# Values of an attention kernel: one wide matmul over the high and low half of the weights, and another order in the first steps

## Chip, cores and metric

One core of a Trainium2 chip. The metric is the device time of one execution in microseconds (us); lower is better. All numbers of this document come from executions on that chip and from a hardware profile of one of them. Engines: PE is TensorE (matmul), PEld its weight loads, DVE VectorE, ACT ScalarE, POOL GpSimd, SP SyncE.

## What is computed

The reference, cut to what matters (4 batches of 512 tokens, model width 512, 16 heads of 128, FFN width 1408, all float32):

```python
xn = layernorm(x)
q = einsum('bpd,hde->bphe', xn, W_Q) + b_Q        # k and v alike
scores = einsum('bqhe,bkhe->bhqk', q, k) / sqrt(128)
attn = softmax(where(causal, scores, -1e5))
z = einsum('bkhe,bhqk->bqhe', v, attn)
s = einsum('bqhe,hed->bqd', z, W_O) + b_O
hdn = silu((xn @ gate_w.T) * gate_s) * ((xn @ up_w.T) * up_s)
g = silu((hdn @ down_w.T) * down_s)
out = x + s * g
```

## The kernel before

**Numbers.** TensorE multiplies in a reduced-width float32 (fp32r). Every operand is therefore kept as a pair: `hi`, the value rounded to fp32r, and `lo`, the rest. A product takes three matmuls, hi·hi, lo·hi and hi·lo, that add into the same PSUM tile (`mm3`, L91, and `mm3_all`, L96). The class `Split` holds such a pair. ACT makes `hi` by a copy that rounds, and DVE or POOL makes `lo` by a subtraction.

**Stages.** First the attention of all heads, then the FFN. The attention loop (L594) goes over 64 steps `n`, in the order group of two heads (`g`, 8 of them), batch (`b`, 4), head in the group (`i`, 2). Everything stands in one order written out by hand (`manual_schedule`), and each engine works its own queue in that order. A step holds, for TensorE: the scores `sc` of this head (`softmax`, L305), a part of side work (`fill`, L607), the projections `psq` and `psk` of the next head (`project`, L278), and `z` = attention times values of the head before (`attend`, L418), then the rest of the side work. The side work at `i == 0` is the values of this group and batch, one tile of 128 tokens at a time (`project_v`, L270, two in the first half of the step, two in the second); at `i == 1` it is the output projection `pso` of the group and batch before (`project_out`, L469).

**Values.** `project_v` makes the 128 tokens times 256 columns (two heads) of a group: 12 matmuls with x's hi or lo as the stationary operand and 256 columns of the weights `wv` as the moving one. Then ACT copies the high half out of PSUM (L274) and DVE subtracts it for the low half (L275). The PSUM tile is one of five buffers of the pool `ps_mm`, which `psq`, `psk`, `z`, `pso` and half of the x transposes `tr` share.

**Softmax.** DVE adds the mask and takes the maximum (L331), ACT takes the exponential (L345), DVE the reciprocal of the sum (L348), POOL multiplies (L351). Then the probabilities are transposed: DVE turns blocks of 32 (L365, `turn_p`), and a trip through DRAM on the SP queue (`turn`, `ptr`) puts the blocks in place. In the next step `split_p` (L387) splits them: ACT makes hi (L398), and the low part is made in two halves (L400), from step 9 on one by POOL and one by DVE.

**Weights.** `prepare` (L176) starts a load and notes when it is due; `split_pending(n)` (L166) splits what is due, by a copy on ACT (L150) and a subtraction on POOL (L151).

**First steps.** Layer norm is `ln_stats` (DVE), `ln_sd` (ACT), `ln_normalize` (DVE) and `ln_transposes`, PE transposes `tr` that are put between the matmuls of `project_v` through the list `side`. Batch 0 is made ahead of the loop, and batch `b + 1` in the second half of the step `(g, i) == (0, 0)` of batch `b`. The statistics of batch 1 are made in two calls, one tile ahead of the loop (L580) and three in step 0 (L661).

**End.** `down` (L792) makes the last projection, 128 tokens at a time, and stores the result on the SP queue. The last tile is made in two halves.

Of the kernel before, what the change touches and what calls it, by code (L numbers as in the profile page):

```python
# [18 lines left out]
P = 128  # L19
# [24 lines left out]
def kernel(  # L44
# [67 lines left out]
    with ExitStack() as at:  # L112
# [70 lines left out]
                prepare(when, flat(d[h]), src[h].rearrange("p c e -> p (c e)"), f"{n}r{h}")  # L183

        def prepare_v(g, due):
            wv[g] = weight(wvop, [P, ND, HG * E], f"wv{g}", "wv")
            half = ND // 2
            for i in range(2):
                c = slice(i * half, (i + 1) * half)
                src = w_v[g][:, c, :].rearrange("p c e -> p (c e)")  # L190
                prepare(due, flat(wv[g][:, c, :]), src, f"wvr{g}_{i}")
# [10 lines left out]
        def ln_stats(b, tt, only=None, mv=None):  # L202

            todo = list(enumerate(tt))
            if only is not None:
                todo = todo[:only] if mv is None else todo[only:]
            if mv is None:
                mv = small.tile([P, len(tt), 2], F32, name="mv")
            for k, t in todo:
                st = small.tile([P, 6], F32, name="st")  # L210
                nc.vector.bn_stats(out=st, in_=x_in[b, t])
                nc.vector.bn_aggr(out=mv[:, k, :], in_=st)
            mv_of[b, tuple(tt)] = mv
            return mv
# [53 lines left out]
        v_of = {}  # L268

        def project_v(g, b, t):  # L270
            ps = ps_mm.tile([P, HG * E], F32, name="psv", tag="mm")
            mm3_all(ps, [(xnT[b][:, c, ts(t, P)], wv[g][:, c, :]) for c in range(ND)])
            v = weight(vp, [P, HG * E], f"v{g}_{b}_{t}", "v")
            nc.scalar.copy(v.hi, ps)  # L274
            nc.vector.tensor_tensor(v.lo, ps, v.hi32, ALU.subtract)  # L275
            v_of.setdefault((g, b), []).append(v)

        def project(b, h, w, bias, name, parts=1):  # L278
# [247 lines left out]
        with tc.manual_schedule():  # L526
# [23 lines left out]
            ln_transpose(0, 1)  # L550
            split_pending(-3)
            wv_lows = split_pending(-2, None)
            mv = ln_stats(0, [2, 3], 1)
            ln_low(0, 0)
            ln_low(0, 1)
            ln_stats(0, [2, 3], 1, mv)
            ln_sd(0, [2, 3])
            table(AF.Exp)
            ln_normalize(0, 2)
# [10 lines left out]
            ln_low(0, 2)  # L570
            ln_low(0, 3)
            project_v(0, 0, 0)
            next(q_of)
            next(k_of)
            qT = next(q_of)
            kT = next(k_of)
            split_pending(-1)
            for t in range(NT):
                load_x(1, t)
            mv = ln_stats(1, range(NT), 1)  # L580
            bo_bc = load_const(b_o.broadcast_to([P, D]), [P, D], "bo_bc")
            ds_bc = load_const(down_s.broadcast_to([P, D]), [P, D], "ds_bc")

# [10 lines left out]
            for n, (g, b, i) in enumerate(heads):  # L594
# [11 lines left out]

                def fill(ks):  # L607
                    for t in ks:
                        if i == 0 and not (n == 0 and t == 0):
                            project_v(g, b, t)  # L610
                        if i == HG - 1 and prev is not None:
                            project_out(*prev, t, zs[prev])
# [7 lines left out]
                of = softmax(qT, kT, norms if n > 0 else [])  # L620
                if n > 1 and early:
                    pt = split_p(raw, B * HG < n < len(heads) - 2)
                if n > 0:
                    while norms:
                        norms.pop(0)()
                look()
                half = NT // 2 if nxt is not None else NT - 1
                fill(range(0, half))
                if nxt is not None:
                    raw_next = turn_p(of)  # L630
                if not early:
# [7 lines left out]
                        load_acc(*prev, t)  # L639
                if nxt is None:  # L640

                    for k, tag in enumerate(("wvh", "wvl")):
                        two = wvop.tile([P, 2, D], F32, name=f"a_last{k}", tag=tag)
                        for t in range(2):
                            load_acc(g, b, 2 * k + t, two[:, t, :])
                per_g = B * HG
                if (b, i) == (0, HG - 1):
                    prepare_o(g, n + 1)
# [9 lines left out]
                    load_look()  # L658
                if nxt is not None:
                    if n == 0:  # L660
                        ln_stats(ln_b, range(NT), 1, mv)  # L661
                    elif ln_b is not None and n != 1:
                        ln_stats(ln_b, range(NT))
                    nh = nxt[0] * HG + nxt[2]
                    *_, qT = project(nxt[1], nh, wq[nh], bq_sb, "q")
                    if n == 0:
                        ln_sd(ln_b, range(NT))
                        table(AF.Exp)
                    while norms:
                        norms.pop(0)()  # L670
                if nxt is not None:
                    *_, kT = project(nxt[1], nh, wk[nh], bk_sb, "k")
                    raw = raw_next
                if before is not None:
                    attend_last(before, pt)
# [5 lines left out]
                if ln_next:  # L681
                    side.extend([lambda: None] * (2 * ND))
                    for t in range(NT):
                        side.extend(ln_transposes(b + 1, t))
                        side.append(lambda t=t: ln_low(b + 1, t))
                    fill(range(half, NT))
                    split_pending(n)
                    while side:
                        side.pop(0)()
                    if b + 2 < B:  # L690
                        for t in range(NT):
                            load_x(b + 2, t)
# [19 lines left out]
    def ffn(exact):  # L712
        with ExitStack() as ff:
# [75 lines left out]
                    nc.sync.dma_start(out=xt, in_=x[b, ts(t, P), :])  # L789
                    tail_in[b, t] = a, xt  # L790

            def down(b, t, parts=1):  # L792
                if not exact:
                    load_tail(b, [t])
                a, xt = tail_in.pop((b, t))
                o = fp.tile([P, D], F32, name="o")
                for k in range(parts):
                    c = ts(k, D // parts)
                    pd = ps_d.tile([P, D // parts], F32, name="pd")
                    for f in range(NF):  # L800
                        w = Split(wd[f].hi[:, c], None if exact else wd[f].lo[:, c])
                        mm(pd, hid[b][f][:, ts(t, P)], w, False, f == 0, f == NF - 1)
                    nc.vector.tensor_tensor(o[:, c], pd, ds_bc[:, c], ALU.mult)  # L803
                    nc.scalar.activation(o[:, c], o[:, c], AF.Silu)  # L804
                    nc.vector.tensor_tensor(o[:, c], o[:, c], a[:, c], ALU.mult)
                    nc.vector.tensor_tensor(o[:, c], o[:, c], xt[:, c], ALU.add)
                    nc.sync.dma_start(out=out[b, ts(t, P), c], in_=o[:, c])

            with tc.manual_schedule():
                for b in range(B):  # L810
                    for f in range(NF):
                        gate_up(b, f)
                        if f == 0 and b > 0:
                            for t in range(NT):
                                down(b - 1, t)
                    if exact:
                        load_tail(b, range(NT))
                for t in range(NT):
                    down(B - 1, t, 2 if t == NT - 1 else 1)

    flag = nc.values_load(inexact, min_val=0, max_val=P * LOW_BITS)
    with tc.If(flag == 0) as cond:
# [62 lines left out]
```

## Time and profile before

| | |
|---|---|
| median of 3 runs | 1213.09 us (1212.78 to 1213.54) |
| the profiled execution | 1212.96 us, of which 1211.2 us lie between its first and last instruction (its span) |
| granted TensorE clock | 0.999 of full speed |
| PE busy | 1198.4 us, 99% of the span |
| DVE, ACT, POOL busy | 792.5, 549.3, 379.1 us (65%, 45%, 31%) |
| values (`psv`) in the chain that ended last | 14% of the span |

A row of a timeline gives the start of a group of equal instructions in us, their time from the first start to the last end, the engine, the line of the kernel, and the tiles. Matmuls are pipelined: one still drains while the next streams, so what a group costs TensorE is the distance from its start to the start of the next group, not its own length. Idle time of an engine and what ended it stands in square brackets.

### The profile page before, as it was taken

The numbers are of one execution on the slowest core, as the hardware profiler recorded it, in microseconds if no ns is written. First come the engines' busy times: TensorE is split into PE (matmuls) and PEld (weight loads), VectorE is DVE, ScalarE is ACT, GpSimd is POOL, SyncE is SP. The second block draws the span as 40 slices with busy tenths as digits, with TensorE's granted clock in tenths as the row PEclk, the third lists the DMA queues.
The fourth block names the chain that finished last, engine by engine and source line by source line (L and its number), as shares of the span: only waits on it lengthen the run. The fifth ranks groups of instructions, "written<-read, shape, count | busy, mean of one in ns | idle before, by whom it ended". The sixth has DMA issues, their size and how long they took to land.

```text
span 1211.2 us, 19214 instructions
## 1 busy us (share of the span) xinstructions
PE 1198.4 (99%) x6466; PEld 1045.7 (86%) x6466; DVE 792.5 (65%) x2149; ACT 549.3 (45%) x1272; POOL 379.1 (31%) x484
## 2 busy tenths in 40 slices
PE   8999999999999999999999999999999999999997
PEld 8888888888888888888888888888888888888886
DVE  7987777777777767777776666667667543443443
ACT  6654444455454445454544454445444331323231
POOL 3222332343234324332523252325231350212010
PEclk9999999999999999999999999999999999999999
DMA  5464455756666667666655555555555892727241
GB/s 180 129 189 155 134 174 191 209 175 199 203 207 197 199 195 220 189 197 194 200 185 180 188 182 174 175 174 182 184 168 168 273 296 79 218 78 223 75 146 38
DMA packets 117913, 215.55 MB, mean 178 GB/s; under 512 B 13232, under 2 KB 45744, under 8 KB 117808
## 3 DMA queue, kind: packets, MB, share of 16 engines
q1 hardware_dynamic: 74016, 134.51, 35.0%
q10 hardware_dynamic: 29376, 53.26, 14.3%
q0 software_dynamic: 14416, 26.48, 8.0%
q8 instruction: 53, 0.87, 0.3%
q14 instruction: 52, 0.43, 0.1%
HBM read 135.17 MB, written 79.04 MB: 177 GB/s over the span
## 4 chain that ended last, share of the span: by engine, by line
PE 94%; issue 2%; DVE 2%; DMA 1%; POOL 1%; ACT 0%; SPq 0%; ACTq 0%; POOLq 0%; DVEq 0%
PE psv L104 14%; PE psq L104 14%; PE psk L104 13%; PE z L432 8%; PE sc L104 8%; PE pd L748 7%; PE pg L748 7%; PE pu L748 7%; PE pso L92 5%; PE pso L93 5%; PE pso L94 5%; PE sc L322 1%; PE z L435 1%; DMA wqr<-in_w_q 1%; DVE sq L365 0%
## 5 line engine op out<-in xcount | busy, mean ns | idle before, releaser
L351 POOL TENSOR_SCALAR p<-p,rtot 128x512 f32<-128x512 f32 (+3 forms) x256 | 149.9, 604 | 591.8 <-DVE rtot L348 570.4
L345 ACT ACTIVATE p<-p,nmax 128x512 f32<-128x512 f32 (+3 forms) x256 | 140.9, 553 | 111.5 <-DVE nmax L331 111.5
L365 DVE STREAM_TRANSPOSE sq<-p 128x256 f32<-128x256 f32 x378 | 113.2, 361 | 0.1
L104 PE MATMUL sc<-k,q 128*128 128x512 f32 (+2 forms) x576 | 111.8, 338 | 0.6 <-ACT k L288 0.6
L104 PEld LDWEIGHTS sc<-k,q 128*128 128x128 f32 x576 | 98.9, 188 | 11.4 <-ACT k L288 0.8
L288 ACT ACTIVATE q<-psq,consts 128x512 fp32r<-128x512 f32 (+1 forms) x65 | 44.4, 682 | 122.4 <-PE psq L104 49.7
L331 DVE CUSTOM_DVE_ANT_0 p<-sc,mask 128x512 f32<-128x512 f32 (+2 forms) x192 | 96.2, 551 | 0.1
L289 DVE SCALAR_TENSOR_TENSOR k<-psk,consts,k 128x512 fp32r<-128x512 f32 (+1 forms) x65 | 48.1, 739 | 72.1 <-ACT k L288 72.1
L400 POOL TENSOR_TENSOR pt<-ptr,pt 128x640 fp32r<-128x640 f32 x53 | 83.6, 1577 | 9.7 <-ACT pt L398 9.5
L398 ACT CAST pt<-ptr 128x640 fp32r<-128x640 f32 x126 | 85.0, 724 | 0.3 <-DMA ptr<-turn 0.2
L288 ACT ACTIVATE k<-psk,consts 128x512 fp32r<-128x512 f32 (+1 forms) x65 | 44.2, 679 | 89.8 <-PE psk L104 89.8
L289 DVE SCALAR_TENSOR_TENSOR q<-psq,consts,q 128x512 fp32r<-128x512 f32 (+1 forms) x65 | 47.9, 737 | 49.2 <-ACT q L288 47.5
L774 DVE SCALAR_TENSOR_TENSOR hd<-pu,consts,sg 128x512 f32<-128x512 f32 x44 | 33.0, 751 | 65.8 <-PE pu L748 61.1
L478 DVE TENSOR_TENSOR a<-pso,a 128x512 f32<-128x512 f32 x108 | 69.4, 681 | 0.0
L348 DVE RECIPROCAL rtot<-tot 128x1 f32<-128x1 f32 x256 | 41.4, 162 | 41.3 <-ACT p L345 35.2
L400 DVE TENSOR_TENSOR pt<-ptr,pt 128x640 fp32r<-128x640 f32 x73 | 66.8, 925 | 0.9 <-ACT pt L398 0.9
L432 PE MATMUL z<-pt,v_0h 128*128 128x512 f32 x128 | 50.5, 394 | 0.0
L345 ACT ACTIVATION_READ_ACCUMULATOR p<-p,nmax 128x1 f32 x256 | 47.9, 187 | 0.0
L432 PE MATMUL z<-pt,v_1h 128*128 128x384 f32 x128 | 44.2, 345 | 0.0
L804 ACT ACTIVATE o<-o 128x512 f32<-128x512 f32 (+1 forms) x17 | 10.3, 607 | 68.8 <-DVE o L803 68.8
L772 ACT ACTIVATE sg<-pg,consts 128x512 f32<-128x512 f32 x44 | 30.3, 688 | 17.4 <-PE pg L748 17.4
L432 PE MATMUL z<-pt,v_2h 128*128 128x256 f32 x128 | 35.9, 280 | 0.0
(758 smaller groups left out, 3270.8 us busy)
## 6 DMA issues: line engine op xcount, KB each, us to landing
turn<-sq SPq DMA_DIRECT2D x63, 640.0 KB, 3.5
ptr<-turn SPq DMA_DIRECT2D x252, 160.0 KB, 3.4
acc<-a SPq DMA_DIRECT2D x124, 256.0 KB, 3.1
a<-acc ACTq DMA_DIRECT2D x108, 256.0 KB, 2.9
xt<-in_x SPq DMA_DIRECT2D x16, 256.0 KB, 4.2
wor<-in_w_o ACTq DMA_DIRECT2D x16, 256.0 KB, 4.6
fa<-acc SPq DMA_DIRECT2D x16, 256.0 KB, 6.4
fx<-in_x SPq DMA_DIRECT2D x16, 256.0 KB, 6.6
```

Source lines behind the costliest of these rows:

```text
L104: nc.tensor.matmul(ps, l, r, start=n == 0, stop=n == len(todo) - 1)
L288: nc.scalar.activation(q.hi[:, at_], ps, AF.Identity, bias=bias[:, h : h + 1])
L289: nc.vector.scalar_tensor_tensor(q.lo[:, at_], ps, bias[:, h : h + 1], q.hi32[:, at_], ALU.add, ALU.subtract)
L331: nc.vector.tensor_tensor_reduce(out=of[t], in0=where[t], in1=add, scale=-SCALE, scalar=BIG, op0=ALU.add, op1=ALU.min, accum_out=nmax[t],)
L345: nc.scalar.activation(of[t], of[t], AF.Exp, bias=nmax[t], scale=-1.0, accum_out=tot)
L351: nc.gpsimd.tensor_scalar(of[t], of[t], rtot, 1.0, ALU.mult, ALU.mult)
L365: nc.vector.transpose(dst.rearrange("p a s i -> p s a i"), src.rearrange("p (s a i) -> p s a i", s=n, i=Q),)
L398: nc.scalar.copy(dst(pt.hi), src)
L400: on.tensor_tensor(dst(pt.lo), src, dst(pt.hi32), ALU.subtract)
L432: nc.tensor.matmul(o, v, p_, start=k == 0, stop=k == len(todo) - 1)
L478: nc.vector.tensor_tensor(a, ps, a, ALU.add)
L748: nc.tensor.matmul(ps, l, r, start=first and k == 0, stop=last and k == len(pairs) - 1)
```

## The change

`project_v` has two forms now. For the first group (`g == 0`) it stays as it was. For the other seven groups, x's hi is multiplied by the hi and lo half of the weights side by side, which makes one matmul of 512 columns, four times (once for each 128 of the model width). The PSUM tile is twice as wide. Then x's lo is multiplied by the weights' hi and added to the first half, four matmuls of 256 columns. ACT copies the second half to SBUF, DVE adds the first half to it, ACT rounds the sum to hi, and POOL subtracts it for lo. For this, hi and lo of `wv` are one tile. The sums take the buffers of the normalized x (`xn`).

Beside this, the order changes in some places. Ahead of the loop: the first two tiles' statistics of batch 1 are made at other places (one of the two comes out of step 0), the loads of batch 1 stand earlier in the text, and the second value tile moves from step 0 to ahead of the first scores. In the steps with layer norm after step 0, the side work of the first half comes ahead of the remaining normalizations. In step 2 (`n == HG`), the split of the first output weights moves from the second half of the value work to just after `psk`. The last step loads its four accumulators into one tile. The last half tile of the output is stored on the ACT queue.

```diff
         def prepare_v(g, due):
-            wv[g] = weight(wvop, [P, ND, HG * E], f"wv{g}", "wv")
+            both = wvop.tile([P, 2, ND, HG * E], F32R, name=f"wv{g}", tag="wv")
+            wv[g] = Split(both[:, 0], both[:, 1])
+            wv[g].both = both
...
         def project_v(g, b, t):
-            ps = ps_mm.tile([P, HG * E], F32, name="psv", tag="mm")
-            mm3_all(ps, [(xnT[b][:, c, ts(t, P)], wv[g][:, c, :]) for c in range(ND)])
             v = weight(vp, [P, HG * E], f"v{g}_{b}_{t}", "v")
-            nc.scalar.copy(v.hi, ps)
-            nc.vector.tensor_tensor(v.lo, ps, v.hi32, ALU.subtract)
+            if g == 0:
+                ps = ps_mm.tile([P, HG * E], F32, name="psv", tag="mm")
+                mm3_all(ps, [(xnT[b][:, c, ts(t, P)], wv[g][:, c, :]) for c in range(ND)])
+                nc.scalar.copy(v.hi, ps)
+                nc.vector.tensor_tensor(v.lo, ps, v.hi32, ALU.subtract)
+            else:
+
+                ps = ps_mm.tile([P, 2, HG * E], F32, name="psv", tag="mm")
+                for c in range(ND):
+                    x_ = xnT[b][:, c, ts(t, P)]
+                    nc.tensor.matmul(ps, x_.hi, wv[g].both[:, :, c, :], start=c == 0, stop=False)
+                for c in range(ND):
+                    x_ = xnT[b][:, c, ts(t, P)]
+                    nc.tensor.matmul(
+                        ps[:, 0], x_.lo, wv[g].hi[:, c, :], start=False, stop=c == ND - 1
+                    )
+                sum_ = lnp.tile([P, D], F32, name="sum", tag="xn")[:, : HG * E]
+                nc.scalar.copy(sum_, ps[:, 1])
+                nc.vector.tensor_tensor(sum_, ps[:, 0], sum_, ALU.add)
+                nc.scalar.copy(v.hi, sum_)
+                nc.gpsimd.tensor_tensor(v.lo, sum_, v.hi32, ALU.subtract)
...
             project_v(0, 0, 0)
+            for t in range(NT):
+                load_x(1, t)
             next(q_of)
             next(k_of)
             qT = next(q_of)
+            mv = ln_stats(1, range(NT), slice(0, 1))
             kT = next(k_of)
             split_pending(-1)
-            for t in range(NT):
-                load_x(1, t)
-            mv = ln_stats(1, range(NT), 1)
+            ln_stats(1, range(NT), slice(1, 2), mv)
+            project_v(0, 0, 1)
...
-                        if i == 0 and not (n == 0 and t == 0):
+                        if i == 0 and not (n == 0 and t < 2):
...
+                look()
+                half = NT // 2 if nxt is not None else NT - 1
+                fill(range(0, half))
                 if n > 0:
                     while norms:
                         norms.pop(0)()
-                look()
-                half = NT // 2 if nxt is not None else NT - 1
-                fill(range(0, half))
...
-                    for k, tag in enumerate(("wvh", "wvl")):
-                        two = wvop.tile([P, 2, D], F32, name=f"a_last{k}", tag=tag)
-                        for t in range(2):
-                            load_acc(g, b, 2 * k + t, two[:, t, :])
+                    a_last = wvop.tile([P, NT, D], F32, name="a_last", tag="wv")
+                    for t in range(NT):
+                        load_acc(g, b, t, a_last[:, t, :])
...
-                        ln_stats(ln_b, range(NT), 1, mv)
+                        ln_stats(ln_b, range(NT), slice(2, NT), mv)
...
                     *_, kT = project(nxt[1], nh, wk[nh], bk_sb, "k")
+                    if n == HG:
+                        split_pending(n)
...
                     fill(range(half, NT))
-                    split_pending(n)
...
-                    nc.sync.dma_start(out=out[b, ts(t, P), c], in_=o[:, c])
+                    (store if k == parts - 1 else nc.sync).dma_start(out=out[b, ts(t, P), c], in_=o[:, c])
...
-                    down(B - 1, t, 2 if t == NT - 1 else 1)
+                    down(B - 1, t, *((2, nc.scalar) if t == NT - 1 else ()))
```

More of the change, by code (lines that the diff above doesn't have):

```diff
@@ L205, in ln_stats @@
             if only is not None:
-                todo = todo[:only] if mv is None else todo[only:]
+                todo = todo[only]
             if mv is None:
@@ L552 @@
             wv_lows = split_pending(-2, None)
[L553 removed]
+            mv = ln_stats(0, [2, 3], slice(0, 1))
             ln_low(0, 0)
             ln_low(0, 1)
[L556 removed]
+            ln_stats(0, [2, 3], slice(1, 2), mv)
             ln_sd(0, [2, 3])
@@ L790, in load_tail, with down @@
                     tail_in[b, t] = a, xt
-            def down(b, t, parts=1):
+            def down(b, t, parts=1, store=nc.sync):
                 if not exact:
```

## Prediction

> **What bounds the kernel now.** I read the page first, then who waits for whom on PE, then timelines of one ordinary value step and of the first steps.
>
> ```profile
> PE 1198.4 (99%) x6466; PEld 1045.7 (86%) x6466; DVE 792.5 (65%) x2149; ACT 549.3 (45%) x1272; POOL 379.1 (31%) x484
> PE 94%; issue 2%; DVE 2%; DMA 1%; POOL 1%; ACT 0%; SPq 0%; ACTq 0%; POOLq 0%; DVEq 0%
> ```
>
> The second line is the chain that ended last, by engine. TensorE is the bound: every other engine idles at least a third of the span. So the change is worth what it takes off TensorE's queue, plus the waits of TensorE that it ends, minus those that it makes. The waits are few:
>
> ```profile
> PE pso L92 <- POOL wo0l L151: 0.7, 2, 0.4
> ...
> PE psv L104 <- DVE v_0l L275: 0.6, 1, 0.6
> PE sc L104 <- ACT k L288: 0.6, 1, 0.6
> PE tr L256 <- DVE xn L239: 0.5, 1, 0.5
> PE tr L256 <- DVE q L289: 0.3, 1, 0.3
> ```
>
> (The waiting tile and whom it waited for: us in total, times, longest.) All of them lie in the first 63 us. After that TensorE is fed by its own queue alone, and a matmul costs the distance to the next one's start:
>
> ```profile
> 255.02 0.22 PE L323 MATMUL sc<-k,q 128*128 128x128 f32 x1
> 255.08 0.69 PE L104 MATMUL psv<-wv2h,xh 128*128 128x256 f32 x4
> 255.61 0.64 PE L104 MATMUL psv<-wv2h,xl 128*128 128x256 f32 x4
> ...
> 258.00 1.09 PE L104 MATMUL psq<-xh,wq5h 128*128 128x512 f32 x4
> 258.93 1.07 PE L104 MATMUL psq<-xh,wq5l 128*128 128x512 f32 x4
> ...
> 260.75 1.07 PE L104 MATMUL psk<-xh,wk5h 128*128 128x512 f32 x4
> ...
> 263.47 0.39 PE L432 MATMUL z<-pt,v_0h 128*128 128x512 f32 x1
> ...
> 269.90 0.45 PE L92 MATMUL pso<-wo1l,z2h 128*128 128x512 f32 x1
> ...
> 270.88 0.39 PE L93 MATMUL pso<-wo1h,z3h 128*128 128x512 f32 x1
> ```
>
> Read starts only. Two value tiles, 24 matmuls of 256 columns, take 258.00 - 255.08 = 2.92 us; in the middle four take 0.48, so 120 ns each. The 12 of psk take 263.47 - 260.75 = 2.72, so 227 ns for 512 columns. Twice the columns cost 1.89 times the time: about 13 ns belong to each matmul, whatever its width.
>
> **The change: the wide matmul.** It removes no column: 12 x 256 = 3072 before, 4 x 512 + 4 x 256 = 3072 after. It removes four matmuls of twelve. With the rows above, a value tile goes from 12 x 120 = 1440 ns to 4 x 227 + 4 x 120 = 1388: 52 to 53 ns less. There are 7 groups x 4 batches x 4 tiles = 112 such tiles: 112 x 53 = 5.9 us at most.
>
> Some of it is lost where narrow matmuls meet wide ones. After the narrow psv, psq takes 260.75 - 258.00 = 2.75, not 2.72, all in its first rows (its first four 0.93, not 0.91). After the 128-column end of the scores, the first four of pso take 270.88 - 269.90 = 0.98 instead of 0.91, while the first four of psv lose only 0.53 - 0.48 = 0.05 there. Before, two value tiles held one such start; after, they hold two (narrow, wide, narrow, wide, narrow). So per pair of tiles 0.02 to 0.03 more at the first start and about 0.02 at the second: 0.106 - 0.05 = 0.056, or 3.1 us over 56 pairs. Inside `z`, where widths change every matmul, one change costs about 10 ns, which would leave 4.8. I take 4.0 (ends 2.9 and 5.9).
>
> A rule speaks against this. The Trainium skill, "TensorE: Matmul & The Clock Gate", section "Back-to-back issue gap", has back-to-back matmuls N/2.4 ns + 2.5 ns apart when warm. By that, a tile goes from 12 x 109.2 = 1310 to 4 x 215.8 + 4 x 109.2 = 1300, and the change is worth 112 x 10 = 1.1 us. But the trace has 120 and 227, not 109 and 216: each matmul here loads new weights, and carries 13 ns, not 2.5. The trace decides.
>
> **Its other engines.** Per tile: before, one ACT copy (0.35) and one DVE subtraction (0.41); after, ACT copies the second half (0.35), DVE adds (0.41, as L275, which also reads PSUM and SBUF), ACT copies from SBUF (about 0.4: L150 has 0.60 for 512 columns), POOL subtracts (estimate 0.65: half of the 1.29 that L151 takes for 512). So ACT gets 112 x 0.4 = 45 us (45% to 49%), POOL 73 us (31% to 37%), DVE nothing. None becomes the bound by sum; what matters is the order. The step of the rows above on the other engines, before:
>
> ```profile
> 257.49 0.35 ACT L274 CAST v_0h<-psv 128x256 fp32r<-128x256 f32 x1
> ...
> 257.69 0.83 DVE L509 TENSOR_TENSOR bits<-bits,look 128x512 int32<-128x512 int32 x1
> ...
> 259.10 0.73 ACT L398 CAST pt<-ptr 128x640 fp32r<-128x640 f32 x1
> 259.11 1.79 DVE L365 STREAM_TRANSPOSE sq<-p 128x256 f32<-128x256 f32 x6
> ...
> 259.28 1.58 POOL L400 TENSOR_TENSOR pt<-ptr,pt 128x640 fp32r<-128x640 f32 x1
> 260.83 0.78 DVE L400 TENSOR_TENSOR pt<-ptr,pt 128x640 fp32r<-128x640 f32 x1
> ```
>
> After, ACT waits for DVE in the middle of this: copy until 257.84; DVE's add behind the look until 258.85; ACT's hi until 259.3; second copy 259.6; second add 260.0; second hi 260.5. Behind it in ACT's queue stand the two casts of pt (now until 261.8), then q's eviction; in DVE's the transposes (until 261.7, 0.9 late), its half of pt, q's low part; in POOL's, its half of pt behind two subtractions (261.2 to 262.8). Here a second rule counts: DVE's half of pt reads two SBUF operands, and where such an operation met POOL, rows differ (the normalization L239 took 0.97 us at 48.29, started together with a POOL operation of 0.69, and 0.55 at 51.98). The Trainium skill, "SBUF — State Buffer", says of the shared port pair that the loser blocks for the whole instruction. By the row DVE's half would end at 262.9, by the rule, behind POOL, at 263.6. I take the later. TensorE needs the high part of pt at z (263.4) and the low part with the third group of z, 1.05 later (264.4). So 1.6 and 0.8 us of cover remain, and nothing is paid. PSUM: psv's buffers are freed by the add at 258.9 and 260.0, and asked for again at 263 or later; q's buffer (free at about 264.3) is asked for by the fourth value tile at about 266.5. The transposes' delay makes the DRAM trip later; it now lands 0.3 to 4.5 us ahead of its cast, so in some steps the cast will wait up to 0.9, and z comes 6 us after it. The sums' buffers are four `xn` buffers, unused after the first group. ACT's queue also holds the accumulator loads behind the second hi: 2 us later, needed a step later. The one wv tile and the one a_last tile: waits go by region (the scores start on k's hi while its lo, in the same tile, is still being made), so nothing.
>
> **First steps.** (1) At 16.43 (psk's last four start at 15.95, and four take 0.48) TensorE has finished psk and waits for its eviction; the scores start at 17.15 and lose another 0.1. The second value tile (1.44 us, psv0's length) now stands there, until 17.87, when k is ready: 0.8 saved. On ACT it adds a 0.35 copy ahead of the exponentials, on DVE 0.42 and one statistic ahead of the first maximum (18.4 to 18.9): 0.5 late, but POOL's first multiplication waits until 21.47 behind two DMA issues anyway. In step 0 two statistics instead of three precede q's low part and xn: 0.8 earlier, which keeps the wait for xn (0.66 in all) as long as it was. The loads of batch 1 stand behind the same loads on SP's queue as before, with the same waits: nothing. But in step 1 DVE waits for the DRAM trip, which does not come earlier, so only 0.46 of it (DVE's idle time at 41.5) reaches step 2. (2) There TensorE waits 0.76 for psv's buffer at 52.69, behind two normalizations; the new order frees it. What is late next is the transpose at 55.58, which waits for q's low part at 56.19, the end of the same DVE work: the gain is taken back. (3) The split of the first output weights moves ahead: POOL's two (2.54 from 59.81) to about 52.5, ACT's two copies (1.15) ahead of z's eviction. The two waits at pso, 0.57 and 0.45, go; POOL beside DVE's normalizations may cost 0.4 there. Sum: 0.5 (0.1 to 0.8) for (1) and (2), 1.1 (0.7 to 1.2) for (3). (4) The last store: issued at 1205.34, landed at 1208.42, 3.1 us; full tiles with nothing before them took 2.0. On ACT's queue, empty then: 0.3 saved (-0.3 to 1.0).
>
> **Sum.** 4.0 + 0.5 + 1.1 + 0.3 = 5.9 us from the profiled execution's 1212.96 (span 1211.2 and 1.8 around it; 0.13 below the median of the runs): 1207.0. All low ends together: 1209.6; all high ends: 1204.1.
>
> **Rivals.**
> A. The round trip stalls TensorE, slower. Place: z in the 28 value steps from group 1 on, waiting for pt's low part. For: two tiles in a row now go ACT, DVE, ACT, POOL through queues that also feed pt, and POOL has been slow beside DVE (at 50.45, 2.32 us for two small multiplications while DVE split pt). Against: the walk above leaves 0.8 us. It decides from 0.8 us of extra delay; at 1.3 each step loses 0.5, 14 us, and the time is 1207.0 + 14 = 1221. Chance 0.07.
> B. Wide matmuls take 240 ns or more in runs of four (psq's first four, 0.93, make 233 each; pso's 0.98 make 245), which is 8 x 120 / 4, the point of no gain. Only the first steps and the store remain, 1.9 us: 1211. Against: psk's 227, and two-piece moving operands (L322: 280 ns long, 283 for one piece) cost nothing. Chance 0.11.
> C. The transitions cost nothing and the first steps give all: 5.9 + 0.8 + 1.2 + 0.5 = 8.4: 1204.6. Chance 0.17.
> D. As summed, 1207.0: 0.65.
>
> **Numbers.** About 0.2% (2.4 us) is what a measurement of this kernel can tell from no change: faster means below 1210.7, slower above 1215.5. D and C are faster, half of B too: 0.87. The other half of B and a touch of stall is the same: 0.07. A, but for its smallest form, is slower: 0.06. The range reaches from just under C to the low ends of D with some of B: 1204.0 to 1209.9.
>
> **What would show it.** PE's matmuls fall by 448. Right: psv pairs at about 2.85 instead of 2.92 in the timeline, the psv share of the chain down, no PE wait after 65 us, waits for k and for wo0l gone, that for xn still there. Wrong: PE waits for pt at z (rival A); psv pairs at 2.92 (B) or 2.81 (C).

## The result, and the profile after

The changed kernel takes 1215.49 us (median of 22 runs, 1214.74 to 1220.65), the kernel before 1213.54 us beside it (22 runs, 1212.78 to 1215.04): a ratio of 1.0019, 95% interval 1.0013 to 1.0025. The change costs 2 us; 1207.0 was forecast, with a range from 1204.0 to 1209.9. The profiled execution is one of two among the 22 that took about 5 us more than the rest (it took 1220.65, its span is 1218.8): in it a single wait of TensorE, shown in the last section, makes up the difference.

From the page of the changed kernel, the busy times and the chain that ended last:

```profile
PE 1197.7 (98%) x6018; PEld 1024.3 (84%) x6018; DVE 822.3 (67%) x2149; ACT 589.3 (48%) x1384; POOL 460.1 (38%) x596
PE 85%; DVE 5%; POOL 4%; ACT 2%; issue 2%; DMA 1%; ACTq 0%; SPq 0%; POOLq 0%; DVEq 0%
```

There are 448 matmuls fewer, as forecast, and ACT and POOL rise to 48% and 38% (49% and 37% were forecast). But the chain, which was 94% TensorE, is now 85%: VectorE, GpSimd and ScalarE have come onto it. The waits of TensorE say where (waiting tile, whom it waited for: us in total, times, longest):

```profile
PE psv L284 <- DVE q L308: 6.4, 6, 1.4
PE z L451 <- DVE pt L419: 3.0, 1, 3.0
...
PE tr L258 <- DVE q L308: 1.3, 1, 1.3
...
PE tr L258 <- DVE xn L241: 0.6, 1, 0.6
PE sc L104 <- DVE q L308: 0.5, 1, 0.5
PE sc L104 <- DVE k L308: 0.2, 1, 0.2
```

The first line is new, and it is what the change costs: a value tile waits for the low part of `q`, six times. The second is the one of this execution alone. The waits for `k` on ScalarE, for `wo0l` and for `v_0l` of before are gone; but the four others shown, all in the first 63 us, come to 2.6 us, and the waits there came to 2.7 before.

The wide matmul itself does what it was meant to do. TensorE's rows of the step whose rows before are shown in the prediction:

```profile
255.98 0.22 PE L342 MATMUL sc<-k,q 128*128 128x128 f32 x1
256.04 1.14 PE L284 MATMUL psv<-wv,xh 128*128 128x512 f32 x4
257.02 0.63 PE L287 MATMUL psv<-wv,xl 128*128 128x256 f32 x4
257.49 1.08 PE L284 MATMUL psv<-wv,xh 128*128 128x512 f32 x4
258.40 0.64 PE L287 MATMUL psv<-wv,xl 128*128 128x256 f32 x4
258.87 1.09 PE L104 MATMUL psq<-xh,wq5h 128*128 128x512 f32 x4
```

Read starts: two value tiles take 258.87 - 256.04 = 2.83 us, and the next pair of this step 2.86 (268.96 - 266.10). So it is in all groups: the median is 2.83 in the first half of a step and 2.86 in the second, 2.845 on average, where it was 2.918. That is 56 x 0.073 = 4.1 us saved.

The account of the first-to-last difference of the two profiled executions, from the starts of TensorE's matmuls in each of the 64 steps (one step is one head of one batch entry): value pairs -4.1; six waits for `q` +7.9; everything up to the scores of step 8 -0.2; the end, from the start of the last matmul to the end of the span, 7.98 before and 6.94 after, -1.0; the single wait for `pt` and its consequences +4.8. Sum 7.4, and the spans differ by 1218.8 - 1211.2 = 7.6. Without the last term it is 2.6, beside 1.95 between the medians.

**Where the six waits come from.** The chain of waits of the changed kernel, around the first of them (step 14; start, us, what):

```profile
228.36 0.34 DVE sum L292
...
228.72 0.41 ACT v_0h L293
...
229.21 0.74 POOL v_0l L294
...
231.08 1.58 POOL pt L419
232.66 1.84 POOL wq4l L151
234.50 1.25 POOL wk4l L151
...
235.77 0.37 ACTq L146
...
236.67 0.70 ACT q L307
...
237.40 0.76 DVE q L308
...
238.20 1.20 PE psv L284 x4
```

Read it from the bottom. The fourth value tile of the step needs the PSUM buffer of `q`. `q` is read out by ScalarE and then by VectorE. But in ScalarE's queue, ahead of `q`, stand the loads of the next group's second q and k weights (`ACTq L146`). They wait for staging buffers that GpSimd's subtractions `wq4l` and `wk4l` still read, and these stand on GpSimd behind `pt`, which stands behind the new rounding of `v`. At the top is the trip: ScalarE copies, VectorE adds, and ScalarE waits for the sum before it can round it, once for each of the two tiles. The same place before, on ScalarE:

```profile
227.93 0.35 ACT L274 CAST v_0h<-psv 128x256 fp32r<-128x256 f32 x1
...
229.10 0.73 ACT L398 CAST pt<-ptr 128x640 fp32r<-128x640 f32 x1
...
234.61 0.34 ACTq L146 DMA_DIRECT2D wkr<-in_w_k  x1
...
235.48 0.69 ACT L288 ACTIVATE q<-psq,consts 128x512 fp32r<-128x512 f32 x1 [3.98 <-POOL wk4l L151]
```

and on TensorE:

```profile
235.86 0.69 PE L104 MATMUL psv<-wv1h,xh 128*128 128x256 f32 x4
...
237.34 0.64 PE L104 MATMUL psv<-wv1h,xh 128*128 128x256 f32 x4
```

ScalarE stood for 3.98 us behind these loads before the change too; TensorE did not feel it, because `q` was out at 236.95 (VectorE's row, 236.20 and 0.75 long) and the fourth tile started at 237.34. The cover, the time between the moment at which a buffer is free and the moment at which it is asked for, was 0.39 us. From ScalarE's first copy to VectorE's start on `q` it was 236.20 - 227.93 = 8.27 us before, and is 237.40 - 227.32 = 10.08 after: 1.81 longer. The pair of tiles ahead of it is 0.07 shorter on TensorE and the tile next to the fourth 0.03, so TensorE asks earlier: 1.81 + 0.07 + 0.03 - 0.39 = 1.5, and the row of the wait has 1.42 us. This constellation occurs once in a group, in steps 14, 22, 30, 38, 46 and 54: the first four wait 1.39 to 1.42 us, the last two 0.43 and 0.36. A row counts a wait from the modelled end of the last matmul; from the start that the fourth tile would have had (236.62, 0.47 us behind 236.15 as in other steps), it is 1.58 us. Against the kernel with the loads moved (below) the six steps are longer by 1.65 to 1.68 us in four, and by 0.69 and 0.62: together 7.9.

### The profile page after: what moved, and what is told of

The parts are those of the page before. It is cut to its first block, busy times and chain, and to the rows that moved or that the text cites. A ratio compares the mean times of both kernels' runs of the same rounds, so it can differ in the third digit from the quotient of the medians.

```text
span 1218.8 us, 18549 instructions
## 1 busy us (share of the span) xinstructions
PE 1197.7 (98%) x6018; PEld 1024.3 (84%) x6018; DVE 822.3 (67%) x2149; ACT 589.3 (48%) x1384; POOL 460.1 (38%) x596
## 4 chain that ended last, share of the span: by engine, by line
PE 85%; DVE 5%; POOL 4%; ACT 2%; issue 2%; DMA 1%; ACTq 0%; SPq 0%; POOLq 0%; DVEq 0%
PE psq L104 12%; PE psk L104 12%; PE z L451 8%; PE psv L284 7%; PE sc L104 7%; PE pd L769 7%; PE pg L769 7%; PE pu L769 7%; PE pso L92 5%; PE pso L94 4%; PE pso L93 4%; PE psv L287 4%; ACT p L364 1%; PE psv L104 1%; POOL pt L419 1%
## 5 line engine op out<-in xcount | busy, mean ns | idle before, releaser
L284 PE MATMUL psv<-wv,xh 128*128 128x512 f32 x448 | 125.3, 401 | 6.4 <-DVE q L308 6.4
L419 DVE TENSOR_TENSOR pt<-ptr,pt 128x640 fp32r<-128x640 f32 x73 | 93.0, 1285 | 2.9 <-ACT pt L417 2.5
L284 PEld LDWEIGHTS psv<-wv,xh 128*128 128x128 f32 x448 | 75.9, 188 | 17.6 <-DVE q L308 7.6
L294 POOL TENSOR_TENSOR v_2l<-sum,v_2h 128x256 fp32r<-128x256 f32 x28 | 20.6, 738 | 151.8 <-ACT v_2h L293 151.8
L292 DVE TENSOR_TENSOR sum<-psv,sum 128x256 f32<-128x256 f32 x112 | 47.1, 421 | 44.0 <-ACT sum L291 42.9
L287 PEld LDWEIGHTS psv<-wv,xl 128*128 128x128 f32 x448 | 68.4, 188 | 9.5
L287 PE MATMUL psv<-wv,xl 128*128 128x256 f32 x448 | 71.0, 280 | 0.0
```

Source lines behind the costliest of these rows:

```text
L284: nc.tensor.matmul(ps, x_.hi, wv[g].both[:, :, c, :], start=c == 0, stop=False)
L287: nc.tensor.matmul(ps[:, 0], x_.lo, wv[g].hi[:, c, :], start=False, stop=c == ND - 1)
L419: on.tensor_tensor(dst(pt.lo), src, dst(pt.hi32), ALU.subtract)
```

## The experiments

Each kernel was timed against the kernel before in five rounds; a ratio stands with its 95% interval. "The change" is the changed kernel.

**The two halves of the change.** First the new order alone, with the narrow matmuls kept; then the new value matmuls alone, in the old order (the kernel before, with `prepare_v`, `project_v` and `a_last` of the change).

```
 def project_v(g, b, t):
-    if g == 0:
+    if g >= 0:
```

> The changed kernel with project_v in its old form for all groups: only the new order, the one wv tile and the store on ACT are left. Theory (the values' round trip pushes q's eviction back in six steps): without the round trip those six waits are gone, and so is the gain of the wide matmul; the first steps leave 0.2 us (scores of step 8 start 0.19 earlier in the profile) and the store 1.0, so about 1212.3 against 1213.5. Rival (the new order of the first steps is what costs): slower than before, 1215 or more.

Measured: 1212.15 against 1213.98 us, ratio 0.9985 (0.9978 to 0.9992). The order is worth 1.8 us (1.0 to 2.7 by the interval). In its profile 0.39 comes from the first steps and 1.0 from the end.

> The kernel before with only the new form of the values (one wv tile, wide matmul, ACT copy, DVE add, POOL subtraction) and the a_last tile that goes with it. Theory: 4.1 us gained by the wide matmul (0.15 per value step, 28 of them) and 8.0 lost in the six steps 14, 22, ... 54: about 1217.4 against 1213.5, and the six PE waits for q's low part in the trace. Rival (the order costs): 4 us faster than before, 1209.5, and no such wait.

Measured: 1218.33 against 1213.98 us, ratio 1.0036 (1.0022 to 1.0049). TensorE's waits hold the same six, and nothing else is new that is as large:

```profile
PE psv L284 <- DVE q L308: 6.9, 6, 1.6
```

So the loss lies in the value matmuls and what follows them on the other engines, not in the order. 4.1 us of matmul time saved and a loss of 4.35 us in the whole leave about 8 us for the waits.

**Is it the loads in ScalarE's queue?** The call that splits and reloads the second q and k weights is moved from ahead of `q`'s projection to just behind `attend_last`, so that `q` is read out before ScalarE comes to these loads. To see whether that is worth something by itself, the same was done to the kernel before.

```
-                    if (b, i) == (B - 1, 0):
-                        prepare_qk((g + 1) * HG + 1, (g + 1) * per_g - 1)
...
                 if before is not None:
                     attend_last(before, pt)
+                if g + 1 < NG and (b, i) == (B - 1, 0):
+                    prepare_qk((g + 1) * HG + 1, (g + 1) * per_g - 1)
```

> The changed kernel, with the loads of the next group's second q and k weights (issued on ACT's queue in the six steps) put behind z's eviction instead of ahead of q's. Theory (ACT's queue stands still at these issues, which wait for staging buffers that POOL's subtractions free, and q's eviction waits behind them): the six waits go, 8.0 us less than the changed kernel: 1207.5. Rival (POOL's or DVE's added work makes q late by itself): the waits stay, 1215.5.

Measured: 1208.00 against 1213.98 us, ratio 0.9947 (0.9933 to 0.9960). The six waits are gone, and nothing has come in their place after 65 us. ScalarE in step 14:

```profile
229.34 0.37 ACT L291 COPY sum<-psv 128x256 f32<-128x256 f32 x1
...
232.81 0.68 ACT L307 ACTIVATE q<-psq,consts 128x512 fp32r<-128x512 f32 x1
...
237.42 0.34 ACTq L146 DMA_DIRECT2D wqr<-in_w_q  x1
```

The trip through VectorE is still as long as in the change; `q` no longer stands behind the loads and is read out at 232.81 instead of 236.67.

> Control: the kernel before, with the same loads put behind z's eviction. Theory (there q's low part ended 0.4 us before TensorE asked for its PSUM buffer, so nothing was lost): no change, 1213.5 to 1214. Rival (late loads are a gain of their own, whatever the values' form): 4 us or more faster, 1209.5.

Measured: 1213.13 against 1213.39 us, ratio 1.0000 (0.9991 to 1.0008). In the kernel before the loads cost nothing where they are. They became dear through the change.

**Is it the trip, or the load on GpSimd?** If GpSimd's 73 us of extra work were the cause, it should help to give the rounding back to VectorE.

```
-                nc.gpsimd.tensor_tensor(v.lo, sum_, v.hi32, ALU.subtract)
+                nc.vector.tensor_tensor(v.lo, sum_, v.hi32, ALU.subtract)
```

> The changed kernel, with v's low part subtracted by DVE instead of POOL. Theory (ACT's wait for DVE between its two copies delays the casts of pt and of the weights by 1.1 us, and POOL's weight subtractions with them): POOL starts its half of pt only when the cast is done, 0.1 to 0.2 us earlier than now, so the six waits shrink by 0.2 us each at most: 1214 to 1215.5. Rival (POOL's two added subtractions per half step push the weights' subtractions back): the six waits go, 1207.5 to 1209.

Measured: 1220.53 against 1213.98 us, ratio 1.0051 (1.0038 to 1.0065). TensorE's waits:

```profile
PE psv L284 <- DVE q L308: 6.6, 6, 1.7
PE z L451 <- DVE pt L419: 2.9, 6, 0.7
```

The first line is as in the change: GpSimd's own work on `v` is not what holds `q` up, since the casts of `pt` come as late without it (230.12 - 227.16 = 2.96 us behind the first copy in step 14, 2.89 in the change), and GpSimd begins its `pt` 3.76 us behind the first copy in both (230.92 - 227.16 here, 231.08 - 227.32 there). The expected time was missed all the same: VectorE, with two more subtractions in the queue, is late with its half of `pt` in the step after each of the six, and these steps are 0.85 to 0.88 us longer than in the kernel with the loads moved in four cases, and 0.41 in two. This is the mechanism of rival A, at its place, but it needs the rounding on VectorE.

**The trip taken out of the way.** The loads stay where the change has them, and so does all the work; only the rounding of `v` (ScalarE's high part and GpSimd's subtraction) waits until the casts of `pt` and the weight splits have been issued.

```
                 nc.vector.tensor_tensor(sum_, ps[:, 0], sum_, ALU.add)
-                nc.scalar.copy(v.hi, sum_)
-                nc.gpsimd.tensor_tensor(v.lo, sum_, v.hi32, ALU.subtract)
+
+                def round_(v=v, sum_=sum_):
+                    nc.scalar.copy(v.hi, sum_)
+                    nc.gpsimd.tensor_tensor(v.lo, sum_, v.hi32, ALU.subtract)
+
+                rounds.append(round_)
...
                     split_pending(n)
+                while rounds:
+                    rounds.pop(0)()
```

> The changed kernel with the loads where they are, but the rounding of the values (ACT's hi, POOL's lo) put behind the casts of pt and of the weights, so that ACT does not wait for DVE between its two copies. Theory (the round trip alone made POOL's weight subtractions 1.1 us late): the six waits fall to 0.2 us at most each, about 1207.5 to 1208.5. Rival (any added work on ACT or POOL is too much ahead of q's eviction): the waits stay, 1214 or more.

Measured: 1207.89 against 1213.39 us, ratio 0.9951 (0.9937 to 0.9965). The six waits are gone. ScalarE in step 14, and GpSimd's `pt`:

```profile
228.05 0.35 ACT L292 COPY sum<-psv 128x256 f32<-128x256 f32 x1
...
229.14 1.36 ACT L422 CAST pt<-ptr 128x640 fp32r<-128x640 f32 x2
...
235.52 0.69 ACT L312 ACTIVATE q<-psq,consts 128x512 fp32r<-128x512 f32 x1 [3.37 <-POOL v_0l L297]
```
```profile
229.96 1.59 POOL L424 TENSOR_TENSOR pt<-ptr,pt 128x640 fp32r<-128x640 f32 x1 [0.17 <-ACT pt L422]
```

From the first copy to the casts of `pt` it is 1.09 us again, as before the change (229.10 - 227.93 = 1.17; in the change 230.21 - 227.32 = 2.89), and VectorE starts on `q` 236.24 - 228.05 = 8.19 us after the copy (8.27 before, 10.08 in the change). With the loads in their place and the same instructions, the wait comes and goes with the trip. So it needs both: the loads ahead of `q`, and the trip ahead of the loads.

**How much of the trip.** Here both copies of a pair come first, then both additions, then both roundings: one trip instead of two in a row.

```
                 nc.scalar.copy(sum_, ps[:, 1])
-                nc.vector.tensor_tensor(sum_, ps[:, 0], sum_, ALU.add)
-                nc.scalar.copy(v.hi, sum_)
-                nc.gpsimd.tensor_tensor(v.lo, sum_, v.hi32, ALU.subtract)
+
+                def finish(v=v, sum_=sum_, ps=ps):
+                    nc.vector.tensor_tensor(sum_, ps[:, 0], sum_, ALU.add)
                    nc.scalar.copy(v.hi, sum_)
                    nc.gpsimd.tensor_tensor(v.lo, sum_, v.hi32, ALU.subtract)
+
+                held.append(finish)
+                if t % 2:
+                    while held:
+                        held.pop(0)()
```

> The changed kernel, but ScalarE copies the second halves of both tiles of a pair first, and only then come the two additions and the two roundings: one trip from ScalarE to VectorE and back in a pair instead of two in a row. Nothing is added or taken away. Theory (the length of the chain ScalarE, VectorE, ScalarE before the casts of pt is what uses up q's cover in steps 14, 22, 30, 38, 46, 54): in step 14 of the changed kernel ScalarE waited 1.06 us for the first sum and 0.49 us for the second; the second wait goes and part of the second copy moves into the first, so the second rounding is done at about 229.5 instead of 230.3, 0.8 us earlier. Of the 8.0 us of TensorE waits for q at psv, 1.5 each in four steps and about 0.55 in two, 0.8 goes in each of the four and 0.55 in the two: 8.0 - 4.3 = 3.7 us stay, and the time is 1215.5 - 4.3 = 1211.2 us. Rival (a trip of any length trips a threshold, for instance because VectorE's transposes or GpSimd's subtractions come in another order): the six waits stay at 1.4 to 1.6 and the time at 1215.5.

Measured: 1213.67 against 1213.12 us, ratio 1.0005 (0.9997 to 1.0014).

```profile
PE psv L286 <- DVE q L317: 4.1, 6, 1.0
```

The waits fell to 0.93 to 1.00 in the four and to 0.17 in the two; in the four that is little more than half of the 0.8 expected. The six steps are 2.3 us shorter than in the change, and 4.3 were expected. GpSimd's rows in step 14 show why:

```profile
229.84 0.75 POOL L298 TENSOR_TENSOR v_0l<-sum,v_0h 128x256 fp32r<-128x256 f32 x1 [0.16 <-ACT v_0h L297]
230.54 0.75 POOL L298 TENSOR_TENSOR v_1l<-sum,v_1h 128x256 fp32r<-128x256 f32 x1
231.25 1.58 POOL L428 TENSOR_TENSOR pt<-ptr,pt 128x640 fp32r<-128x640 f32 x1
```

In the change the two subtractions lay in the gaps of the trip, and GpSimd's `pt` began 0.15 us after ScalarE's first cast was done (230.93). Here they stand back to back, and `pt` begins behind the second, 0.52 us after the first cast is done (230.00 and 0.73 long). ScalarE's chain is shorter, GpSimd's has taken over. VectorE starts on `q` 237.54 - 227.95 = 9.59 us after the first copy, 1.32 longer than before. By the sum used above, 1.32 + 0.07 + 0.03 - 0.39 = 1.03, and the wait in this step is 0.93 (in the change 1.5 by the sum and 1.42 in the row). Three lengths of the chain and one cover so give three waits: 8.19 and none, 9.59 and 0.93, 10.08 and 1.42. So the six steps explain 2.0 (4.3 - 2.3) of the 2.5 us by which the expected 1211.2 us was missed.

**The first steps.** In step 2 of the change VectorE's last normalization lies beside the split of the first output weights, which was moved there (VectorE's row, then GpSimd's):

```profile
53.11 1.32 DVE L241 TENSOR_SCALAR xn<-xt,mv,rstd 128x512 f32<-128x512 f32 x1
```
```profile
52.85 2.72 POOL L151 TENSOR_TENSOR wo0l<-wor,wo0h 128x512 fp32r<-128x512 f32 x2 [0.55 <-ACT wo0h L150]
```

To the kernel with the late loads one edit was added: that split goes to the end of step 1, where GpSimd idles.

> The changed kernel with the loads behind z's eviction, and the split of the first output weights moved from step 2 to the end of step 1, where POOL is idle. Theory for the first steps (POOL's split slowed one of DVE's normalizations in step 2 from 0.55 to 1.32 us, and q's low part with it, on which a transpose waits): DVE's normalization is back at 0.55, 0.5 to 0.9 less than with late loads alone: 1207.1 to 1207.5. Rival (the transpose waits for something else): 1208.

Measured: 1206.81 against 1213.39 us, ratio 0.9950 (0.9936 to 0.9964). GpSimd splits at 41.13 now, and the normalization is short again:

```profile
52.37 0.55 DVE L241 TENSOR_SCALAR xn<-xt,mv,rstd 128x512 f32<-128x512 f32 x1
```

Step 2 is 1.14 us shorter than in the kernel with the late loads alone, and TensorE's wait for `q` at the transposes falls from 1.4 to 0.8. The spans are 1204.0 and 1206.5, but 0.5 us of this difference lies ahead of step 0, where both kernels are the same. Against the kernel before, the two ratios (0.9950 and 0.9947) cannot be told apart: the shorter step is seen in the profiles, not in the medians. With its 6.6 us it is the lowest median of the study, and it beats both kernels.

To it a second edit was added: the loads of two constants (`bo_bc` and `ds_bc`), issued on GpSimd's queue, go into step 0, behind the store that begins the softmax's trip through DRAM.

> The last one, and the two constant loads of POOL's queue moved behind the first softmax, so that POOL's first multiplication does not stand behind them (21.60, with the sums ready at 21.1). Theory (step 1 hangs on the first trip through DRAM, which starts after that multiplication): 0.3 to 0.5 us less than with the output weights early, 1206.7 to 1207.2. Rival: the trip starts no earlier, no difference.

Measured: 1209.15 against 1213.39 us, ratio 0.9960 (0.9946 to 0.9973): no gain, and a median 2.3 us above that of the version without it. The DMA issues between 17 and 34 us (KB each, median us to landing), without the second edit and with it:

```profile
turn<-sq SPq DMA_DIRECT2D x1, 640.0 KB, 2.9
```
```profile
turn<-sq SPq DMA_DIRECT2D x1, 640.0 KB, 4.9
...
bo_bc<-in_b_o POOLq DMA_DIRECT2D x1, 256.0 KB, 4.1
```

The store that begins the trip through DRAM is issued 0.3 us earlier, as expected (23.61 instead of 23.91), but it lands later, with the two loads beside it: ScalarE's first cast of `pt` comes at 33.86 instead of 31.95. Steps 1 and 2 are 1.4 and 1.3 us longer, and the scores of step 3 start at 60.22 instead of 57.82. More than half of that is not waiting but clock. TensorE's row where its waits begin, and two stretches behind them (of each engine busy time and instructions; then the granted clock, DMA share, GB/s):

```profile
40.77 0.49 PE L104 MATMUL sc<-k,q 128*128 128x512 f32 x1 [1.23 <-ACT k L307]
```
```profile
42.40:45.80 3.40, 3.35 (x13) 3.25 (x14) 3.30 (x8) 1.22 (x1) 2.00 (x2) 0.50 0.52 185
45.80:49.20 3.40, 3.40 (x26) 3.25 (x26) 2.66 (x14) 2.89 (x6) 0.11 (x1) 1.00 0.63 142
```

At half the clock, 3.4 us do the work of 1.7. Four of the five executions of this kernel had a mean clock of 0.997 and took 1208.18 to 1209.34 us; the fifth had 0.999 and took 1207.40, which is 0.6 above the median without the edit. A load that was free in its place was not free in another, and by this profile most of its price was the clock.

**The last store.** The version of 1206.8 us, with the last half tile stored from SyncE's queue as before.

```
-                    down(B - 1, t, *((2, nc.scalar) if t == NT - 1 else ()))
+                    down(B - 1, t, 2 if t == NT - 1 else 1)
```

> The best version so far (loads of the next group's second weights late, first output weights split at the end of step 1; 1206.8 us), with the second half of the very last output tile stored from SyncE's queue again, as in the kernel before. Theory (the store is no faster on ScalarE's queue, but SyncE's last waits no longer stand behind it): from the last matmul to the end of the span 7.9 instead of 6.9 us, and 1207.8 us in all. Rival (the 1.0 us at the end came from the last output tile, not from the queue): 1206.8 us, and the tail stays at 6.9.

Measured: 1208.44 against 1213.12 us, ratio 0.9959 (0.9945 to 0.9972). From the start of the last matmul to the end of the span it is 8.5 us instead of 6.8. The ratios of the two versions (0.9959 and 0.9950) overlap in their intervals, so this reading rests on the profiles; they agree. In the eight profiled executions with the last store on ScalarE's queue this stretch takes 6.4 to 7.6 us, in the four with it on SyncE's queue 8.0 to 9.1. So it is the queue that brings the gain at the end: 1.7 us here, 1.0 between the change and the kernel before.

## Why the prediction was wrong, point by point

**The matmul.** Right: 4.0 us forecast, 4.1 measured; pairs at 2.85, as forecast. Its choice between the two ways of reading a transition held, and rivals B and C (2.92 and 2.81) are out. So the trace was the right guide against the rule on back-to-back matmuls too: 1.1 us by the rule, 4.1 in the trace. The section that it cites (the Trainium skill, "TensorE: Matmul & The Clock Gate", "Back-to-back issue gap") calls this formula the gap of an isolated matmul, without a weight load for each.

**The other engines: the step that failed.** The prediction walked one step through the queues, the step at 255 us, and found: "q's buffer (free at about 264.3) is asked for by the fourth value tile at about 266.5" and "nothing is paid". For this step the walk was right. In the profile of the change the step begins 0.96 us later; with that taken off, the second high part ends at 260.42 (forecast 260.5), GpSimd's half of `pt` at 262.78 (262.8), VectorE's half at 263.46 (263.6, the later of the two ends that the prediction weighed, 0.68 behind GpSimd's), `q`'s buffer is free at 264.12 and asked for at 266.59. (The row that was set against the later end, a normalization, reads one tensor and not two.) What failed is that one step stood for all 28. In the step it took, no q and k weights are split or loaded; `q` follows the casts at once and has 2.5 us of cover. In the last batch entry of each group, ScalarE's queue holds two loads that wait for GpSimd, `q` stands 4 us behind them, and the cover was 0.39 us; a chain that got 1.81 us longer used it up, and six steps together paid 7.9 us where the prediction had nothing. The row that says so was in the trace of before (`[3.98 <-POOL wk4l L151]` ahead of `q`), and no wait of TensorE pointed to it, because the cover was just enough. The question that leads there is which DMA issues stand on ScalarE's queue in each kind of step, and what each of them waits for.

**Rival A.** It had the mechanism (two tiles in a row go through ScalarE, VectorE, ScalarE and GpSimd, "through queues that also feed pt") but put the place at `z` in 28 steps. The place that is paid is `psv`, through `q`, in six. Its size, 14 us, came from the 28; the runs show 7.9.

**First steps.** Forecast 0.5 for the wait for `k` and for psv's buffer and 1.1 for the split of the output weights; the profile has 0.2 for all, at step 8. The waits for `k` and `wo0l` went, as forecast: 0.66 and 1.19 us. What was mis-sized is the price in step 2: "POOL beside DVE's normalizations may cost 0.4" was 1.32 - 0.55 = 0.77 in one of them, and the whole step got 1.23 longer, with 1.3 us of waiting for `q` at the transposes. That this wait would take back what the free psv buffer gave was forecast. Another 0.37 was lost in step 4. The wait for `xn` stayed, as forecast.

**Last store.** Forecast 0.3 us, because an empty queue would be faster. It is not: issued at 1213.99, the store took 3.5 us to land, and 3.1 before. Yet the end came 1.0 us sooner, since most of SyncE's closing waits no longer begin after it (last section). Together with the first steps the order was forecast at 1.9 us and measured at 1.8. That is luck: the first steps brought less than forecast and the store more, and the two errors cancel.

**The sum.** 1207.0 was forecast; the change with its six waits removed takes 1208.0 with the loads moved and 1207.9 with the rounding moved. Of the 8.5 us between forecast and result, the waits are 7.5 (1215.49 - 1208.00), or 7.9 if each kernel is taken against the kernel before beside it (1.95 slower and 5.98 faster). Without the waits, the forecast of 5.9 us came out in sum: 6.0 and 5.5.

**What stays open.** Why the medians of the change and of the kernel before differ by 1.95 us, when the terms of the profile without the single long wait sum to 2.6, stays open. One profiled execution of each can't settle it: the scores of step 0 start between 17.69 and 18.82 us in the eight kernels that have the text of the change up to there. So the 0.2 us of the first steps is not firm either. Two more staging buffers, which would free the loads without moving them, were not tried.

## What to carry to other kernels

An instruction that issues a DMA stands in its engine's queue like any other: if it waits for a buffer, all compute behind it waits as well (here `q` stood 4 us behind two loads). So the cover of a chain has to be worked out for every variant of a step, with the rare loads in it, and the smallest cover decides; a cover that is just enough shows no wait in the profile. When two stretches in one queue can each be moved past the other (the loads behind `q`, or the rounding behind the casts), either move frees the path, and neither removes work.

## What the runs showed of the hardware

**Who wins between VectorE and GpSimd.** VectorE's half of `pt`, with two operands in SBUF, takes 0.78 us undisturbed. In the profiled execution of the change, once, it met four GpSimd subtractions in a row (VectorE's row, then GpSimd's):

```profile
721.51 5.50 DVE L419 TENSOR_TENSOR pt<-ptr,pt 128x640 fp32r<-128x640 f32 x1
```
```profile
721.30 2.58 POOL L151 TENSOR_TENSOR wv<-wvr,wv 128x512 fp32r<-128x512 f32 x2
723.81 1.30 POOL L151 TENSOR_TENSOR wq13l<-wqr,wq13h 128x512 fp32r<-128x512 f32 x1
725.03 1.29 POOL L151 TENSOR_TENSOR wk13l<-wkr,wk13h 128x512 fp32r<-128x512 f32 x1
```

It ended at 727.01, 0.69 us after the last of them (726.32). The Trainium skill, "SBUF — State Buffer", says under "SBUF: two separate sides" that the shared port pair is held for the whole instruction and the other side blocks. The trace agrees and goes further: VectorE did not get in between the four subtractions either. In step 14 of the change it did: its half of `pt` (231.59, 1.75 us long) met GpSimd's half, and ended 0.68 us after it, beside GpSimd's next subtraction. What decides between the two cases no run here shows.

**The clock after a gap.** That delay left TensorE idle for 2.96 us, from 724.19 to 727.15. The gap and what followed, in the columns used above:

```profile
724.20:727.20 3.00, 0.05 (x1) 0.08 (x1) 3.00 (x2) 0.00 (x0) 2.13 (x2) 1.00 0.51 132
727.20:730.60 3.40, 3.40 (x10) 2.92 (x11) 2.23 (x5) 1.14 (x3) 0.00 (x0) 0.50 0.34 76
730.60:734.00 3.40, 3.40 (x18) 2.95 (x18) 2.53 (x6) 0.11 (x2) 0.00 (x0) 1.00 0.20 77
```

For 3.4 us after the gap the clock was at 0.50, which is another 1.7 us of work, and the step lost 4.8 us, not 3.0. After the first of the six waits (1.42 us, between 236 and 240) it stayed at 1.00. But the version with the constants in step 0 had the same 3.4 us at 0.50 after waits of 1.23, 0.53 and 0.16 us with single matmuls between them, in which TensorE was busy for 1.0 of 2.8 us (39.6 to 42.4). So waits of TensorE can cost more than their length, and the longest single wait alone does not tell when.

**The end of the program.** SyncE closes with a row of twelve waits. With the last store on its own queue these begin when the store has landed (1208.71 in the kernel before, landing 1208.42), and the span ends at 1211.2, 2.8 us after the landing. With the store on ScalarE's queue nine of them run while the store is under way (1214.50 to 1215.05 in the change); the store lands at 1217.48, and the span ends 1.3 us later. The row accounts for only part of the difference: it takes 0.7 us in the kernel before. A pause of 1.2 us between SyncE's last instructions there (1209.69 to 1210.87) has no counterpart above 0.5 us in the change, and no run shows what it is.
